# Softmax sums by f16 matmuls over each head's partitions, and four elementwise steps on GpSimd

## The chip, the cores and the metric

The kernel runs on one core of a Trainium2 chip. A core has a matrix engine (TensorE, PE in the profile), a vector engine (VectorE, DVE), an activation engine (ScalarE, ACT), GpSimd (POOL) and a queue that issues the DMAs (SyncE, SP). The metric is the device time of one execution in microseconds, less is better. The time before is the median of three runs, 1120.3 us.

## The reference

Eight sequences of 512 tokens, model width 512, 16 heads of 32, feed-forward width 2048. All inputs and outputs are float32. Cut to what matters:

```python
xn = layernorm(x)                       # over the last axis
q, k, v = heads(xn @ Wq.T), heads(xn @ Wk.T), heads(xn @ Wv.T)
q, k = rope(q), rope(k)
scores = einsum('bhqd,bhkd->bhqk', q, k) / sqrt(32), causal
attn = softmax(scores)                  # exp, divided by its sum over the keys
ctx = einsum('bhqk,bhkd->bhqd', attn, v)
s = ctx @ Wo.T
h = gelu(bitlinear(xn, w_fc))           # ternary weights
g = silu(bitlinear(h, w_proj))
out = x + s * g
```

The change is in the division by the softmax's sums.

## The kernel before

Work comes in units: 8 sequences x 4 groups of four heads make 32 units of attention (`attn(n)`), and 32 tiles of 128 tokens of the feed-forward part (`ffn`, then `out_tile`). The attention of unit n runs like this:

- `pqk`, 24 f16 matmuls (the inputs are split into an f16 hi and an f16 lo part, three products for each), then the rotation on VectorE into `r` (lines 842 to 847), its rounding `rh` on ScalarE and the rest `rl` on VectorE (851, 852). SP stores both through DRAM (`dq`, `dk`) and loads them back as stacked operands `qst` and `kst` (856 to 864).
- `pm`, 16 matmuls per unit for the row maxima. VectorE reduces them with a mask (line 886, `scr` in the profile), and the shifts go back into `qst`.
- `scores(kb)`, four blocks of 128 keys: `psc` matmuls, the exponential on ScalarE into the f32 tile `p{kb}` (four heads, only the queries from the block on), and the causal mask of its first 128 columns on GpSimd (`affine_select`, line 918). Keys are on the partitions, queries along the free axis.
- `weigh(kb)`: f32 matmuls of `v` (32 columns for each head) with `p{kb}` add up the context `cps` in a PSUM bank. The heads of a group lie at partitions 0, 32, 64 and 96 (`tile_position`).
- Gather (938 to 940): VectorE adds p1, p2 and p3 into p0, so that p0 holds, for every query, 128 partial sums. ScalarE copies `cps` to the SBUF tile `cu` (942).
- Sum (944 to 962): f32 matmuls of p0 with `sel`, 128 columns at a time, set the sums of the four query blocks into four rows of each head's 32 partitions, so that `sps` is 128 x 128. One reciprocal over 128 columns; its f16 hi and lo parts `rx`; eight f16 matmuls with `bsel` spread them over the head's partitions into `pbc` (128 x 512); VectorE multiplies `cu` by it.
- `chl` (964 to 967): the context's f16 hi part on ScalarE and lo part on VectorE, for the output matmuls `po` of `out_tile`.

The feed-forward part gives TensorE most of its work: `pf` (up), a gelu on ScalarE, `ghl` (hi and lo parts, ScalarE and VectorE), a transposing DMA `gT`, and `py` (down). `F` is the gate, `xr` the residual input and at last the output (line 1046, an addition on VectorE).

The order of the program isn't the order of the text. A planner (`Plan`) records every operation as a node with a cost (function `cost`) and a priority (`KEYS`, plus the unit's number), runs a list scheduling over the five engines, and emits the instructions in order of their planned starts. So every engine has a fixed order when it runs, and all instructions come from one line (439) in the profile; they are told apart by their tiles. `plan.join` makes one node of several matmuls. Its model of VectorE and GpSimd lengthens a GpSimd instruction that starts while VectorE runs one with two SBUF inputs (lines 380 to 384); a VectorE instruction isn't lengthened there by GpSimd.

Tiles come from pools with a fixed number of buffers: p0 to p3, `r`, `rh`, `rl`, `cu` and `rr` have one each, `cps` and `sps` one PSUM bank each, and six banks rotate for the other matmuls.

Of the kernel before, what the change touches and what calls it, by code (L numbers as in the profile page):

```python
# [21 lines left out]
P = 128  # L22
# [19 lines left out]
RBITS = 1597463007.0  # L42

KEYS = dict(
    e0=-0.253,
    e1=-2.644,
    e2=-1.78,
    e3=-0.65,
    e4=-0.087,
    e5=-0.039,  # L50
    lag=1.963,
    const0=-24.54,
    const1=-8.335,
    cst=-4.513,
    load=-2.111,
    stats=-22.226,
    norm=-1.897,
    factor=-4.454,
    wload=-1.833,
    wstep=1.494,  # L60
    weight=-19.388,
    balance=-4.407,
    wo=4.918,
    wfsum=-21.116,
    wf=-7.624,
    wp=-0.05,
    wpload=-1.337,
    wpsum=-14.152,
    tstep=0.06,
    proj=-0.686,  # L70
    rope=-24.912,
    hilo=-1.795,
    stack=-34.848,
    v=0.652,
    max=-0.869,
    shift=0.633,
    score=0.129,
    kstep=0.195,
    weigh=1.36,
    gather=1.125,  # L80
    sum=0.848,
    ctx=-41.941,
    up=-0.708,
    fstep=0.123,
    split=-0.465,
    root=0.15,
    down=0.339,
    gate=0.454,
    out=5.344,
    load0=-15.402,  # L90
    stats0=-12.949,
    norm0=-6.181,
    wload0=-7.484,
    weight0=-7.258,
    balance0=-15.07,
    wfload=-7.712,
)
TUNE = dict(table=5.421, margin=0, dma_margin=1734, reserve=0, window=2.34, wide=0.886, backlog=10530.0)

# [361 lines left out]
def cost(eng, op, out, ins, a, k):  # L461
    n, psum = out.n, any(x.store.where == "PSUM" for x in ins)
    if op == "dma_start":
        size = n * out.shape[0] * SIZE[out.dtype]
        t = 1310 if k.get("transpose") else 660 if size <= 16384 else 520
        return t, t, None
    if op == "matmul":
        m, n = ins[0], ins[1].n
        if SIZE[ins[1].dtype] == 4:
            t = n * 0.42 + 10 if m.n <= 32 else n * 4 / 2.4 + 20  # L470
        else:
            t = max(n / 2.4 + 2.5, 27.0)
        return t, t + 170, None
    if op == "transpose":
        return 110, 300, None
    if eng == "ACT":
        f = ins[0].n
        d = (160 if psum else 186) + 0.833 * f + 55 * (psum and f in (256, 384)) + 93 * sum(isinstance(k.get(q), View) for q in ("bias", "scale"))
        table = TABLE.get(a[2]) if op == "activation" else None
        if "accum_out" in k:  # L480
            return d + 100, d + 200, table
        return d - 95, d, table
    if eng == "POOL":
        full = sum(x.n == n for x in ins)
        if n <= 8:
            d = 110 if op == "memset" else 195 + 90 * (op == "tensor_scalar" and len(ins) > 1)
        elif op == "affine_select":
            d = 90 + 1.57 * n
        elif op == "memset":
            d = 100 + 0.84 * n  # L490
        else:
            d = 190 + 2.25 * n if full > 1 else 200 + 1.5 * n
        return d - 40, d, None
    if op == "tensor_tensor_reduce":
        d = 233 + 1.047 * n
    elif op == "reciprocal":
# [15 lines left out]
def block_kernel(  # L512
# [33 lines left out]
    def ps(shape, name, dt=F32):  # L546
        return pp(shape, dt, tag="ps", name=name)
# [18 lines left out]
    ones = cp([P, P], F32, name="ones")  # L566
    ident16 = cp([P, P], F16, name="ident16")
    mask = cp([P, S], BF16, name="mask")
    sel = cp([P, NT, DK], F32, name="sel")
    bsel = cp([P, NT, P], F16, name="bsel")  # L570
    kst = [cp([P, HG, S], F16, name=f"kst{i}") for i in range(2)]
    qst = [cp([P, HG, S], F16, name=f"qst{i}") for i in range(2)]
    rnd = cp([P, 2], F32, name="rnd")

    def constants():
        at("const0")
        ident = wk([P, P], F32, tag="rr", name="ident", bufs=1)
# [14 lines left out]
        for i in range(2):  # L592
            G.memset(kst[i][96:98].rearrange("p h s -> p (h s)").bitcast(F32), MSC2)
        G.memset(sel, 0.0)
        G.memset(sel[:, :, NT:], 1.0)
        for qb in range(NT):
            G.memset(sel[:, qb, qb : qb + 1], 1.0)
        G.memset(bsel, 1.0 / RSC)
        for qb in range(NT):
            v = bsel[:, qb, :].rearrange("p (j d) -> p j d", d=DK)  # L600
            G.affine_select(
                out=v, in_=v, pattern=[[-DK, HG], [0, DK]],
                compare_op=ALU.is_equal, fill=0.0, base=-qb, channel_multiplier=1,
            )
        at("cst")
        SP.dma_start(cst, cs.rearrange("t p s -> p t s"))

# [3 lines left out]
    def ln(b, ts):  # L611
# [25 lines left out]
        for i, t in enumerate(ts):  # L637
# [4 lines left out]
            tag, nb = ("hl", 3) if b else ("gT", 4)  # L642
            hl = wk([P, 2, D], F16, tag=tag, name=f"xhl{b}_{t}", bufs=nb)
            A.copy(hl[:, 0], xt)
            V.tensor_tensor(hl[:, 1], xt, hl[:, 0], ALU.subtract)
            flip(xT[b][:, :, :, t * P : (t + 1) * P], hl)
        at("factor", base)
        fs = wk([P, NT], F32, tag="fs", name=f"fs{b}_{ts[0]}", bufs=8)[:, 0:k]
# [45 lines left out]
    def out_weight():  # L694
# [21 lines left out]
        pb = pc([P, P], F32, tag="sps", name="pom2")[:, 0:2]  # L716
        T.matmul(pb, ones[0:1, :], r, start=True, stop=True)
        V.tensor_copy(cwo, pb)
        hi, lo = wo_s
# [12 lines left out]
    def tern_scale(which, acc, n):  # L732
        a1 = wk([P, 1], F32, tag="acc1", name=f"acc1{which}", bufs=2)
        V.tensor_reduce(a1, acc[:, 0:n], AX.X, ALU.add)
        pt = pc([P, P], F32, tag="sps", name=f"pacc{which}")[:, 0:1]
# [52 lines left out]
    def tern_down():  # L788
# [22 lines left out]
        ones16 = wk([P, P], F16, tag="rx", name="ones16", bufs=1)  # L811
        G.memset(ones16, 1.0)
        for i, w in enumerate(ws):
            at("wp", tstep=i)
# [9 lines left out]
    def attn(n):  # L824
# [24 lines left out]
        rh = wk([P, 2, S], F16, tag="rh", name=f"rh{n}", bufs=1)  # L849
        rl = wk([P, 2, S], F16, tag="rl", name=f"rl{n}", bufs=1)  # L850
        A.copy(rh, r)
        V.tensor_tensor(rl, r, rh, ALU.subtract)
        at("stack", n)
        q_, k_ = qst[n % 2], kst[n % 2]
        dqk = []
# [48 lines left out]
            )  # L904
        cps = pc([P, S], F32, tag="cps", name=f"cps{n}")
        isc = 1.0 / math.sqrt(DK)
        pts = {}

        def scores(kb):
            at("score", n, kstep=kb)  # L910
            w = S - kb * P
            pt = wk([P, HG, w], F32, tag=f"p{kb}", name=f"p{kb}_{n}", bufs=1)
            pts[kb] = pt
            for h in range(HG):
                p = ps([P, S], f"psc{n}_{kb}_{h}")
# [29 lines left out]
        for qb in range(NT):  # L945
# [12 lines left out]
        pb = ps([P, NT, P], f"pbc{n}")  # L958
        for qb in range(NT):
# [72 lines left out]
    def out_tile(b, t):  # L1032
# [71 lines left out]
```

## Time and profile before

| | |
|---|---|
| three runs | 1118.4, 1120.3, 1120.6 us |
| the profiled execution | 1119.6 us |
| its span, from the first to the last instruction | 1117.9 us |
| mean granted TensorE clock | 0.995 |

Where one unit's sums and division spend their time (mean of one instruction, from the groups by form):

| engine | instruction | in all | mean ns |
|---|---|---|---|
| PE | `sps`, f32 records, 32 x 128 columns | 1024 | 279 |
| PE | `pbc`, f16, 128 columns | 256 | 219 |
| PE | `cps`, f32 records, 512 / 384 / 256 / 128 columns | 1024 | 593 / 487 / 379 / 273 |
| VectorE | gather, 1536 / 1024 / 512 elements | 96 | 1778 / 1243 / 682 |
| VectorE | reciprocal, 128 x 128 | 32 | 955 |
| VectorE | `rx` hi / lo | 64 | 218 / 292 |
| VectorE | `cu` times `pbc` | 32 | 677 |
| VectorE | `rl` (1024) / `ch` (512) / `xhl` (512) / `xr` (512) | 128 | 1219 / 691 / 702 / 691 |
| ScalarE | copy of `cps` | 32 | 572 |
| GpSimd | causal mask of `p` | 512 | 422 |

How to read it: the profile lists, for each engine, how long its instructions ran. Matmuls overlap each other, so a record's own length (279 ns) is more than what it adds to the stream. An f32 matmul leaves two records, an f16 one a single record. Some matmul records can be missing.

### The profile page before, as it was taken

What the parts mean: (1) busy time and instruction counts of PE and PEld (TensorE: products, weight loads), DVE (VectorE), ACT (ScalarE), POOL (GpSimd) and SP (SyncE); (2) the same over time, 40 slices, a digit from 0 to 9 for tenths busy, and PEclk for the clock granted to TensorE, in tenths of its full rate; (3) what the DMA queues carried; (4) which work ended last, traced back from release to release, by engine and by line L of the source; (5) the groups of instructions that cost most, each with busy time, mean ns of one, the idle gap of its engine ahead of it and who ended that gap; (6) DMA issues with size and microseconds to landing.
All of it is one profiled execution on the core that took longest, in us unless ns stands there. A gap on an engine that the chain in (4) does not pass through costs nothing.

```text
span 1117.9 us, 23834 instructions
## 1 busy us (share of the span) xinstructions
PE 1077.2 (96%) x8118; PEld 559.3 (50%) x8118; DVE 881.3 (79%) x2187; ACT 698.9 (63%) x1519; POOL 533.6 (48%) x1661
## 2 busy tenths in 40 slices
PE   1899999999999999999999999999999999999998
PEld 0444554555455555455555455555455555545553
DVE  7999898987887777967787777886788777786754
ACT  6858865675566655567556557665557665555763
POOL 6487725542573336543363444643448333344452
PEclk9989999999999999999999999999999999999999
DMA  9875654553455434554545335452345543324423
GB/s 284 286 159 130 124 127 120 109 110 72 112 130 114 100 88 110 96 102 105 115 113 114 70 84 143 105 133 76 76 105 126 122 100 81 81 61 98 105 58 104
DMA packets 233178, 127.15 MB, mean 114 GB/s; under 512 B 191840, under 2 KB 208224, under 8 KB 233056
## 3 DMA queue, kind: packets, MB, share of 16 engines
q1 hardware_dynamic: 233056, 125.63, 48.2%
q8 instruction: 64, 1.05, 0.4%
q14 instruction: 58, 0.48, 0.1%
HBM read 55.05 MB, written 25.17 MB: 72 GB/s over the span
## 4 chain that ended last, share of the span: by engine, by line
PE 82%; DVE 8%; DMA 3%; POOL 3%; issue 2%; SPq 1%; ACT 1%; DVEq 0%
PE py L439 19%; PE pf L439 15%; PE pqk L439 13%; PE po L439 7%; PE pv L439 6%; PE psc L439 6%; PE pm L439 6%; PE cps L439 6%; PE sps L439 3%; POOL hu L439 2%; PE pbc L439 1%; POOL rs L439 1%; DMA wn<-in_wqk 1%; DVE p L439 1%; DVE r L439 1%
## 5 line engine op out<-in xcount | busy, mean ns | idle before, releaser
L439 PE MATMUL py<-wp,gT 128*128 128x512 f16 x1024 | 301.2, 379 | 0.0
L439 POOL TENSOR_SCALAR_AFFINE_SELECT p<-p 128x128 f32<-128x128 f32 x512 | 203.5, 422 | 115.4 <-ACT p L439 109.3
L439 ACT ACTIVATE p<-psc 128x256 f32<-128x256 f32 (+3 forms) x512 | 179.4, 450 | 118.8 <-PE psc L439 118.4
L439 PEld LDWEIGHTS <-xT 128*128 128x128 f16 x2560 | 186.4, 98 | 122.3 <-issue 11.1
L439 PE MATMUL pf<-wf,xT 128*128 128x512 f16 x1024 | 239.5, 380 | 1.3 <-ACT wf L439 1.3
L439 DVE CUSTOM_DVE_ANT_0 scr<-pm,mask 128x128 f16<-128x128 f32 (+3 forms) x512 | 221.3, 486 | 19.7 <-PE pm L439 18.4
L439 POOL TENSOR_TENSOR sq<-sq 128x1 f32<-128x1 f32 (+2 forms) x128 | 45.3, 354 | 346.8 <-ACT ghl L439 341.7
L439 PE MATMUL pqk<-xT,wqk 128*128 128x512 f16 x768 | 175.7, 382 | 0.0
L439 DVE TENSOR_TENSOR p<-p,p 128x1536 f32<-128x1536 f32 (+2 forms) x96 | 118.5, 1234 | 71.5 <-PE cps L439 61.1
L439 ACT CAST rh<-r 128x1024 f16<-128x1024 f32 x32 | 33.4, 1045 | 184.9 <-DVE r L439 179.6
L439 PEld LDWEIGHTS <-gT 128*128 128x128 f16 x1024 | 98.0, 97 | 94.8 <-issue 7.7
L439 DVE SCALAR_TENSOR_TENSOR ghl<-g,rng,ghl 128x512 f16<-128x512 f32 x128 | 95.5, 748 | 52.6 <-ACT ghl L439 50.9
L439 PE MATMUL pm<-kst,qst 96*128 96x128 f16 (+3 forms) x512 | 121.1, 303 | 2.7 <-DVE mm L439 0.9
L439 PE MATMUL psc<-qst,kst 98*128 98x256 f16 (+3 forms) x512 | 118.1, 299 | 0.4 <-DVE mm L439 0.2
L439 PEld LDWEIGHTS <-wqk 128*128 128x128 f16 x768 | 74.5, 99 | 86.7 <-issue 4.8
L439 ACT ACTIVATE g<-pf,fs 128x512 f32<-128x512 f32 x128 | 87.3, 683 | 36.7 <-PE pf L439 33.7
L439 PE MATMUL pv<-wv,xT 128*128 128x128 f16 x1536 | 95.3, 220 | 2.0 <-DMA wv<-whl 1.9
L439 ACT ACTIVATE ghl<-g,sq 128x512 f16<-128x512 f32 x128 | 91.6, 715 | 0.8 <-POOL sq L439 0.7
L439 ACT ACTIVATE ghl<-g,rng 128x512 f16<-128x512 f32 x128 | 91.5, 716 | 0.1
L439 PE MATMUL po<-wo,ch 128*128 128x512 f16 x384 | 88.3, 379 | 0.0
L439 ACT ACT_TABLE_LOAD x64 | 82.1, 1283 | 2.8 <-PE psc L439 1.0
L439 PE MATMUL cps<-p,v 128*32 128x512 f32 (+3 forms) x1024 | 83.3, 433 | 0.0
(141 smaller groups left out, 1343.7 us busy)
## 6 DMA issues: line engine op xcount, KB each, us to landing
qst<-dq SPq DMA_DIRECT2D x96, 128.0 KB, 3.0
kst<-dk SPq DMA_DIRECT2D x96, 128.0 KB, 3.1
xt<-in_x SPq DMA_DIRECT2D x32, 256.0 KB, 3.5
xr<-in_x SPq DMA_DIRECT2D x32, 256.0 KB, 3.0
out<-xr SPq DMA_DIRECT2D x32, 256.0 KB, 2.5
dq<-rh SPq DMA_DIRECT2D x32, 128.0 KB, 2.4
dk<-rh SPq DMA_DIRECT2D x32, 128.0 KB, 2.5
dq<-rl SPq DMA_DIRECT2D x32, 128.0 KB, 2.6
```

The costliest lines, as they stand in the source:

```text
L439: ins = getattr(self.real[nd.eng], op)(*[real(x) for x in a], **{q: real(x) for q, x in k.items()})
```

## The change

It does six things. (1) The sums are taken with a constant `tot` of 128 x 32, all 1/1024, over all 512 queries at once, so that each of a head's 32 partitions gets the same sum, divided by 1024 in the weight and multiplied by 1024 in the operand. For that the gathered p0 is split, in two halves of 256 queries, into an f16 hi part (ScalarE) and an f16 lo part (VectorE), which are put into the memory of p1 and p2; eight f16 matmuls add them up in `sps`, now 128 x 512. (2) The reciprocal runs over 512 columns and its result is what the context needs in each partition, so `rx`, `bsel` and `pbc` go. (3) The context is read from PSUM in the product, and the copy of `cps` goes. (4) Four steps go from VectorE to GpSimd: `rl`, the lo part of the context, the lo part `xhl` of the normalized input (for all sequences but the first), and the last addition into `xr`. (5) The planner's cost of an f16 matmul with 32 columns or fewer is a quarter of the former. (6) All priorities in `KEYS` and most values of `TUNE` are new, so that the order of the whole program is another. The constants `sel` and `bsel` are gone, and some small tiles lie under other tags.

```diff
-TUNE = dict(table=5.421, margin=0, dma_margin=1734, reserve=0, window=2.34, wide=0.886, backlog=10530.0)
+TUNE = dict(table=2.939, margin=1, dma_margin=1441, reserve=1, window=2.34, wide=0.883, backlog=15949.0)
...
-            t = max(n / 2.4 + 2.5, 27.0)
+            t = max(n / 2.4 + 2.5, 27.0) if m.n > 32 else max(n / 9.6 + 1.0, 27.0)
...
-    sel = cp([P, NT, DK], F32, name="sel")
-    bsel = cp([P, NT, P], F16, name="bsel")
+    tot = cp([P, DK], F16, name="tot")
...
+        G.memset(tot, 1.0 / RSC)
...
-            V.tensor_tensor(hl[:, 1], xt, hl[:, 0], ALU.subtract)
+            (G if b else V).tensor_tensor(hl[:, 1], xt, hl[:, 0], ALU.subtract)
...
-        V.tensor_tensor(rl, r, rh, ALU.subtract)
+        G.tensor_tensor(rl, r, rh, ALU.subtract)
...
-            pt = wk([P, HG, w], F32, tag=f"p{kb}", name=f"p{kb}_{n}", bufs=1)
+            raw[kb] = wk([P, 2 * HG * w], F16, tag=f"p{kb}", name=f"p{kb}_{n}", bufs=1)
+            pt = raw[kb].bitcast(F32).rearrange("p (h w) -> p h w", h=HG)
...
-        cu = wk([P, S], F32, tag="cu", name=f"cu{n}", bufs=1)
-        A.copy(cu, cps)
         at("sum", n)
-        sps = pc([P, P], F32, tag="sps", name=f"sps{n}")
-        for qb in range(NT):
-            plan.join = True
+        ahl = [raw[kb][:, 0 : HG * S].rearrange("p (h w) -> p h w", h=HG) for kb in (1, 2)]
+        for i in range(2):
+            hs = slice(i * S // 2, (i + 1) * S // 2)
+            A.activation(ahl[0][:, :, hs], pts[0][:, :, hs], AF.Copy, scale=RSC)
+            V.scalar_tensor_tensor(ahl[1][:, :, hs], pts[0][:, :, hs], RSC, ahl[0][:, :, hs], ALU.mult, ALU.subtract)
+        sps = pc([P, S], F32, tag="sps", name=f"sps{n}")
+        plan.join = True
+        for a in range(2):
             for h in range(HG):
                 T.matmul(
-                    sps[DK * h : DK * h + DK, :], sel[:, qb, :], pts[0][:, h, qb * P : (qb + 1) * P],
-                    start=(qb == 0), stop=(qb == NT - 1), tile_position=(0, DK * h),
+                    sps[DK * h : DK * h + DK, :], tot, ahl[a][:, h, :],
+                    start=(a == 0), stop=(a == 1), tile_position=(0, DK * h),
                 )
-            plan.join = None
-        rr = wk([P, P], F32, tag="rr", name=f"rr{n}", bufs=1)
+        plan.join = None
+        rr = wk([P, S], F32, tag="rr", name=f"rr{n}", bufs=1)
         V.reciprocal(rr, sps)
-        rx = wk([P, 2, P], F16, tag="rx", name=f"rx{n}", bufs=1)
-        V.tensor_scalar(rx[:, 0], rr, RSC, None, ALU.mult)
-        V.scalar_tensor_tensor(rx[:, 1], rr, RSC, rx[:, 0], ALU.mult, ALU.subtract)
-        pb = ps([P, NT, P], f"pbc{n}")
-        for qb in range(NT):
-            for a in range(2):
-                T.matmul(pb[:, qb, :], bsel[:, qb, :], rx[:, a], start=(a == 0), stop=(a == 1))
-        V.tensor_tensor(cu, cu, pb.rearrange("p a b -> p (a b)"), ALU.mult)
+        cu = wk([P, S], F32, tag="cu", name=f"cu{n}", bufs=1)
+        V.tensor_tensor(cu, cps, rr, ALU.mult)
...
-        V.tensor_tensor(chl[:, 1], cu, chl[:, 0], ALU.subtract)
+        G.tensor_tensor(chl[:, 1], cu, chl[:, 0], ALU.subtract)
...
-        V.tensor_tensor(xr, xr, F, ALU.add)
+        G.tensor_tensor(xr, xr, F, ALU.add)
```

More of the change, by code (lines that the diff above doesn't have):

```diff
@@ L44 @@
 KEYS = dict(
[L45 to L96, printed above, removed]
+    e0=-0.291,
+    e1=-2.232,
+    e2=-1.64,
+    e3=-0.189,
+    e4=-0.61,
+    e5=-0.034,
+    lag=2.012,
+    const0=-25.636,
+    const1=-9.365,
+    cst=-1.613,
+    load=-2.107,
+    stats=-18.101,
+    norm=-1.942,
+    factor=-0.587,
+    wload=-1.573,
+    wstep=1.536,
+    weight=-13.751,
+    balance=-3.455,
+    wo=4.776,
+    wfsum=-12.771,
+    wf=-6.783,
+    wp=-0.441,
+    wpload=-1.703,
+    wpsum=-3.384,
+    tstep=0.106,
+    proj=-0.618,
+    rope=-24.134,
+    hilo=-15.6,
+    stack=-28.295,
+    v=0.349,
+    max=-0.824,
+    shift=0.779,
+    score=0.142,
+    kstep=0.252,
+    weigh=0.16,
+    gather=0.681,
+    sum=1.245,
+    ctx=-37.701,
+    up=-0.632,
+    fstep=0.095,
+    split=-0.497,
+    root=0.632,
+    down=0.369,
+    gate=1.588,
+    out=5.026,
+    load0=-23.925,
+    stats0=-11.953,
+    norm0=-5.714,
+    wload0=-7.222,
+    weight0=-7.314,
+    balance0=-29.165,
+    wfload=-7.848,
 )
-TUNE = dict(table=5.421, margin=0, dma_margin=1734, reserve=0, window=2.34, wide=0.886, backlog=10530.0)
+TUNE = dict(table=2.939, margin=1, dma_margin=1441, reserve=1, window=2.34, wide=0.883, backlog=15949.0)
 SIZE = {F16: 2, BF16: 2, F32: 4, I32: 4}
@@ L576, in constants @@
         at("const0")
-        ident = wk([P, P], F32, tag="rr", name="ident", bufs=1)
+        ident = wk([P, S], F32, tag="cu", name="ident", bufs=1)[:, 0:P]
         G.memset(ident, 0.0)
@@ L593, in constants @@
             G.memset(kst[i][96:98].rearrange("p h s -> p (h s)").bitcast(F32), MSC2)
-        G.memset(sel, 0.0)
-        G.memset(sel[:, :, NT:], 1.0)
-        for qb in range(NT):
-            G.memset(sel[:, qb, qb : qb + 1], 1.0)
-        G.memset(bsel, 1.0 / RSC)
-        for qb in range(NT):
[L600 to L604, printed above, removed]
+        G.memset(tot, 1.0 / RSC)
         at("cst")
@@ L715, in out_weight @@
         V.reciprocal(r[:, 1:2], r[:, 0:1])
-        pb = pc([P, P], F32, tag="sps", name="pom2")[:, 0:2]
+        pb = pc([P, S], F32, tag="sps", name="pom2")[:, 0:2]
         T.matmul(pb, ones[0:1, :], r, start=True, stop=True)
@@ L734, in tern_scale @@
         V.tensor_reduce(a1, acc[:, 0:n], AX.X, ALU.add)
-        pt = pc([P, P], F32, tag="sps", name=f"pacc{which}")[:, 0:1]
+        pt = pc([P, S], F32, tag="sps", name=f"pacc{which}")[:, 0:1]
         T.matmul(pt, ones, a1, start=True, stop=True)
@@ L810, in tern_down @@
         tern_scale(1, acc, NW)
-        ones16 = wk([P, P], F16, tag="rx", name="ones16", bufs=1)
+        ones16 = wk([P, S], F16, tag="scr", name="ones16", bufs=2)[:, 0:P]
         G.memset(ones16, 1.0)
@@ L906, in attn @@
         isc = 1.0 / math.sqrt(DK)
-        pts = {}
+        pts, raw = {}, {}
         def scores(kb):
@@ L940, in attn @@
             V.tensor_tensor(acc, acc, pts[kb], ALU.add)
-        cu = wk([P, S], F32, tag="cu", name=f"cu{n}", bufs=1)
-        A.copy(cu, cps)
         at("sum", n)
-        sps = pc([P, P], F32, tag="sps", name=f"sps{n}")
-        for qb in range(NT):
-            plan.join = True
+        ahl = [raw[kb][:, 0 : HG * S].rearrange("p (h w) -> p h w", h=HG) for kb in (1, 2)]
[6 more added lines that the diff above has]
+        for a in range(2):
             for h in range(HG):
                 T.matmul(
-                    sps[DK * h : DK * h + DK, :], sel[:, qb, :], pts[0][:, h, qb * P : (qb + 1) * P],
-                    start=(qb == 0), stop=(qb == NT - 1), tile_position=(0, DK * h),
-                )
-            plan.join = None
-        rr = wk([P, P], F32, tag="rr", name=f"rr{n}", bufs=1)
+                    sps[DK * h : DK * h + DK, :], tot, ahl[a][:, h, :],
+                    start=(a == 0), stop=(a == 1), tile_position=(0, DK * h),
+                )
+        plan.join = None
+        rr = wk([P, S], F32, tag="rr", name=f"rr{n}", bufs=1)
         V.reciprocal(rr, sps)
-        rx = wk([P, 2, P], F16, tag="rx", name=f"rx{n}", bufs=1)
-        V.tensor_scalar(rx[:, 0], rr, RSC, None, ALU.mult)
-        V.scalar_tensor_tensor(rx[:, 1], rr, RSC, rx[:, 0], ALU.mult, ALU.subtract)
-        pb = ps([P, NT, P], f"pbc{n}")
-        for qb in range(NT):
-            for a in range(2):
-                T.matmul(pb[:, qb, :], bsel[:, qb, :], rx[:, a], start=(a == 0), stop=(a == 1))
-        V.tensor_tensor(cu, cu, pb.rearrange("p a b -> p (a b)"), ALU.mult)
+        cu = wk([P, S], F32, tag="cu", name=f"cu{n}", bufs=1)
+        V.tensor_tensor(cu, cps, rr, ALU.mult)
         at("ctx", n)
```

## The prediction

> **What bounds the kernel now.** I read the page first: busy shares, then the chain that ended last.
>
> ```profile
> PE 1077.2 (96%) x8118; PEld 559.3 (50%) x8118; DVE 881.3 (79%) x2187; ACT 698.9 (63%) x1519; POOL 533.6 (48%) x1661
> ...
> PE 82%; DVE 8%; DMA 3%; POOL 3%; issue 2%; SPq 1%; ACT 1%; DVEq 0%
> ```
>
> A busy TensorE need not be at its peak, so I asked for windows of 100 us (columns: window, length, then busy us of PE, PEld, DVE, ACT and POOL).
>
> ```profile
> 300.00:400.00 100.00, 99.26 (x758) 51.66 (x757) 78.99 (x196) 61.92 (x136) 48.61 (x155) 1.00 0.45 99
> 900.00:1000.00 100.00, 100.00 (x766) 52.67 (x765) 73.43 (x179) 59.58 (x132) 37.67 (x123) 1.00 0.37 88
> ```
>
> From 200 us to 1000 us PE loses at most 0.7 us in 100, and the granted clock is 1.00. TensorE's own stream is the bound: an instruction less on PE shortens the run, and a wait of PE lengthens it. Next, the PE timeline of one unit (start, length of a group of alike instructions; the next group's start tells what it occupied).
>
> ```profile
> 613.03 0.86 PE L439 MATMUL sps<-p,sel 128*32 128x128 f32 x24
> 613.71 0.83 PE L439 MATMUL cps<-p,v 128*32 128x256 f32 x16
> 614.48 1.47 PE L439 MATMUL pf<-wf,xT 128*128 128x512 f16 x6
> ...
> 627.91 0.43 PE L439 MATMUL sps<-p,sel 128*32 128x128 f32 x8
> 628.15 1.69 PE L439 MATMUL cps<-p,v 128*32 128x512 f32 x16
> 629.77 0.34 PE L439 MATMUL psc<-qst,kst 98*128 98x128 f16 x3
> ```
>
> The f32 work lies in two batches: 1.45 us for 384 sps and 384 cps columns (each of four heads), 1.86 us for 128 and 896. The difference gives 0.41/256 = 1.60 ns a column, and 0.22 us is left over per batch, which I take as the price of entering and leaving it. Last, what a long GpSimd instruction does to VectorE; before the change the only such ones in the attention part are the weights' lo parts, whl.
>
> ```profile
> 101.37 1.42 POOL L439 TENSOR_TENSOR whl<-wn,whl 128x512 f16<-128x512 f32 x1 [1.58 <-ACT wn L439]
> 101.76 1.57 DVE L439 SCALAR_TENSOR_TENSOR ghl<-g,rng,ghl 128x512 f16<-128x512 f32 x1
> ...
> 103.26 0.68 DVE L439 TENSOR_TENSOR p<-p,p 128x512 f32<-128x512 f32 x1
> ...
> 103.99 0.30 PE L439 MATMUL sps<-p,sel 128*32 128x128 f32 x2 [0.77 <-DVE p L439]
> ```
>
> That ghl has a mean of 748 ns; here it took 1.57 us and ended 0.5 us after whl. The gather behind it on VectorE came late, and PE stood 0.77 us at sps. At 111.99 a second ghl lasted 1.40 us behind a whl, while mask reductions, which read PSUM, ran beside another whl at 0.55 and 0.69 us. So what waits is VectorE's work with two SBUF inputs.
>
> **The change, part by part** (32 units of batch and head group).
>
> PE removes. The sums: 512 columns x 1.60 = 0.82 us. The broadcast pbc: 0.06 + 0.39 us in the timeline, 0.45. Together 1.27 us a unit, 40.7 us.
>
> PE adds eight f16 matmuls of 512 columns, 32 wide. No row has this form. Far bound above: one after another as the wide ones (12 in 2.59 us, so 0.216 each), 1.73 us. Nearer: the f32 records of cps, eight to four heads, follow each other every 0.10 us though one of 512 columns lasts 593 ns, so the column groups run side by side; f16 needs one record where f32 has two, which bounds a group of four at 0.41 us. Below, one wide matmul, 0.216. I take 0.22, two groups, 0.44 us a unit, 14.1 us (to 55). Batches: in the order of the built kernels, runs of f32 matmuls rise from 75 to 97, since cps now comes in three pieces, and 32 runs of f16 sums join them: 54 x 0.22 = 11.9 us (from 0). PE's sum: -40.7 + 14.1 + 11.9 = -15 us, between -27 and +27.
>
> VectorE loses, by mean rows: rl 1.22, xhl 0.70 (28 tiles), ch 0.69, xr 0.69, the 128-wide reciprocal 0.96, both rx 0.51, the cu product 0.68: 5.4 us. It gains two hi/lo subtractions of 1024 elements (row rl, 1.22 each), the product from PSUM (0.68), and a reciprocal of 512. Its bounds: 0.96 (no growth) and 3.8 (four times the row); the rows of 1 element (152 ns) and of 128 (955) give 6.3 ns an element, 3.4 us, which I take. Net +1.1 us, so about 36 us more on 881: some 81% of the span, no bound by itself. ScalarE loses the cu copy (0.57) and gains two copies of 1024 (rh's row, 1.05): +49 us, 66%, hidden by its idle time (it waits 180 us for r); without that cover, 1.5 us a unit.
>
> GpSimd gains rl, ch, xhl and xr, 124 instructions. From whl (median 1157 ns at 512) and z (220 ns at one element): 1.16 us each, rl 2.1 us; +173 us, 63% of the span. Behind rl on its queue stand the sq and z steps, which the gate needs much later. SP's loads of qst and kst stand behind the dq and dk stores of rl, which land perhaps 1 to 2 us later; pm follows r by 12 us today and is what would be late. The output's DMA follows xr by 0.5 us; th waits for its buffer (3.3 us in all today).
> The sel and bsel constants leave GpSimd's start, where it waits 6.5 us for wn anyway: nothing.
>
> What GpSimd's long instructions cost VectorE is the unknown. In the built order, two of four units run: last gather, first subtraction, second subtraction, reciprocal, with ScalarE doing rh ahead of the second half's copy. Counting from the end of r: gather to 0.6, subtraction to 1.75; rh to 1.05, copy to 2.1. rl wants to start at 1.1, gets in at about 1.7 and runs to 3.8. The second subtraction, ready at 2.1, starts at 3.7: 1.6 us late. Then sps is late, on which PE stands, and reciprocal, ghl and the masks are queued behind it on VectorE. The reciprocal is ordered ahead of a ghl that is ready some 2.4 us after that copy (ScalarE's g, 0.68 + 0.19, its Square, 0.72 + 0.19, its copy, 0.72, one running into the next), so the plan has at most 0.5 us of room at sps: 1.1 us a unit, 16 units, 18 us. In the other two, rl falls under the reciprocal or under the statistics of the next batch, which have one input: 0. The last xhl of a batch comes behind the last masks, where the gathers are: 0.9 us in 8 units, 7 us. ch and xr fall under masks: 0. Bounds: 0 if all is covered; by the whl rows (1.3 us of PE waits for p, from three such instructions after 100 us), 0.43 us x 156 lengths of 512 = 68 us. I take 25, nearer to the lower end, because the order shows where they fall; 1150 in the range stands for 45.
>
> The Trainium skill, "SBUF — State Buffer", section "SBUF: two separate sides", calls the port pair of VectorE and GpSimd an exclusive lock: whichever starts first holds it for its whole instruction. The rows above show the wait, but ghl came through at 0.82 and 0.65 us extra, parts of a whl. By the rule taken at its worst, every one of the 156 lengths would cost its full 1.16 us of VectorE, 181 us, and the run would pass 1280; by the rows it is the 25 above.
>
> Sum: the profiled execution took 1119.6 us (span 1117.9), 0.7 under the median. 1117.9 - 15 + 25 = 1128 us of span, 1130 as a median.
>
> **The rivals.**
> 1. Faster: the waits are covered and only PE's saving counts. For it: DVE idles 20 us in 100, and PE chooses among plenty of matmuls of the feed-forward part. Against: the order is fixed when built, and it already puts sps where its input comes. 1120.3 - 15 = 1105; with 5 us of waits or the batches at nothing, 1094 to 1110. It decides where PE loses under 0.47 us a unit (15/32).
> 2. Even: waits near 15 us, 1118 to 1122.5.
> 3. The f16 column groups don't run side by side: PE +27 us, 1147, and more with waits. The overlapping f32 records speak against it.
> 4. The long reciprocal: sps to cu grows by 2.4 us and the single cps bank is held until then. By the built order the next cps starts about 10 us of PE work after sps, against some 5.5 us of reciprocal, ghl and product; 1 us a unit beyond that gives 1105 + 32 = 1137.
>
> **How the numbers follow.** Forecast (waits over 17 us, up to 45: 1122.5 to 1150) 0.45; rival 1, 0.38; rival 2, 0.07; rivals 3 and 4, 0.05 each. What a measurement can tell from no change is about 0.2%, 2.2 us. Slower 0.45 + 0.05 + 0.05 = 0.55, same 0.07, faster 0.38. The range must reach into rival 1: 1095 to 1150, leaving out about 0.2; the forecast's own range is 1122.5 to 1150.
>
> **What would show it.** Right: pbc gone and eight sps records a unit in about 0.5 us; PE waiting at sps for p (some 1 us, in half of the units), with a subtraction of 2.5 us or more beside rl; PE idle of 2 to 3 us in 100. Wrong: PE as dense as before and a batch's period, now 133.0 us (pqk at 464.22 and 597.20), shorter by 1.8 us; or sps taking 1.7 us; or VectorE's two-input instructions at their old durations beside rl, which would take the whole price away.

## The result and the profile after

| | before | after |
|---|---|---|
| median of four runs each | 1119.35 us | 1135.3 us |
| lowest to highest | 1118.07 to 1120.6 | 1134.91 to 1136.52 |
| span of the profiled execution | 1117.9 us | 1133.2 us |
| mean granted TensorE clock | 0.995 | 0.993 |

The ratio is 1.0144, with a 95% interval of 1.0127 to 1.0162: slower by 1.4%. The page of the profile after, in the two lines shown of before (busy time by engine, then the chain that ended last by engine):

```profile
PE 1068.3 (94%) x7094; PEld 516.6 (46%) x7094; DVE 967.7 (85%) x2063; ACT 753.6 (67%) x1553; POOL 734.5 (65%) x1775
...
PE 66%; DVE 15%; POOL 7%; ACT 4%; DMA 4%; issue 3%; SPq 1%; POOLq 0%; DVEq 0%; ACTq 0%
```

TensorE works 8.9 us less, as meant, and the run is 15.3 us longer. VectorE, with 15% of the chain instead of 8%, and GpSimd, with 7% instead of 3%, now end more of the waits. The two windows of 100 us that were shown of before (window, length, busy PE, PEld, DVE, ACT, POOL, clock):

```profile
300.00:400.00 100.00, 98.09 (x664) 47.94 (x663) 87.20 (x183) 67.00 (x143) 70.27 (x169) 1.00 0.49 112
900.00:1000.00 100.00, 100.00 (x710) 50.15 (x708) 84.43 (x171) 64.97 (x137) 55.17 (x136) 1.00 0.40 95
```

The late window is as dense as before; the early one lost 1.2 us more. The groups by form show what the new instructions cost (form, count, then total us and mean ns, then idle time of the engine ahead of them):

```profile
L439 DVE RECIPROCAL rr<-sps 128x512 f32<-128x512 f32 x32 | 107.3, 3353 | 8.7 <-PE sps L439 8.5
L439 PE MATMUL sps<-p,tot 128*32 128x512 f16 x256 | 21.8, 389 | 5.2 <-DVE p L439 3.2 <-ACT p L439 2.0
L439 DVE SCALAR_TENSOR_TENSOR p<-p,p 128x1024 f16<-128x1024 f32 x64 | 99.5, 1565 | 5.6 <-ACT p L439 5.2 <-PE cps L439 0.2
L439 POOL TENSOR_TENSOR rl<-r,rh 128x1024 f16<-128x1024 f32 x32 | 81.3, 2542 | 103.7 <-ACT rh L439 103.7
L439 POOL TENSOR_TENSOR ch<-cu,ch 128x512 f16<-128x512 f32 x32 | 43.9, 1372 | 46.1 <-ACT ch L439 46.1
```

The wide reciprocal is 3.35 us, the eight f16 matmuls overlap (256 of them are 21.8 us busy), and the subtraction of 1024 elements is longer in the mean than the 1.22 us that the same size took before: some of these instructions were held up. PE's timeline of a unit (start, length) has the pattern that was forecast, with a wait for p in the middle of the sums, but a short one:

```profile
633.40 0.40 PE L439 MATMUL sps<-p,tot 128*32 128x512 f16 x4
634.01 0.40 PE L439 MATMUL sps<-p,tot 128*32 128x512 f16 x4 [0.21 <-DVE p L439]
634.35 1.47 PE L439 MATMUL po<-wo,ch 128*128 128x512 f16 x6
```

Where was the time lost? The starts of the reciprocals serve as marks, one for each unit of attention:

| stretch, between the reciprocals' starts (units counted from 0) | before | after | difference |
|---|---|---|---|
| start to unit 0 | 104.5 us | 122.4 us | +17.9 |
| unit 0 to unit 8 | 242.9 | 248.1 | +5.1 |
| unit 8 to unit 24, four batches | 532.5 (133.1 a batch) | 528.0 (132.0 a batch) | -4.5 |
| unit 24 to unit 31 | 214.9 | 212.2 | -2.7 |
| unit 31 to the end | 23.1 | 22.5 | -0.6 |

All of the loss, 23.0 us, lies ahead of unit 8, in the first two of the eight batches. The steady batches, for which the prediction's sum was made, became shorter by 1.1 us. PE's longest waits of the whole run (us in all, times, longest):

```profile
PE pacc L439 <- DVE acc L439: 22.0, 1, 22.0
PE po L439 <- POOL ch L439: 7.1, 5, 1.7
PE pf L439 <- ACT wf L439: 4.9, 1, 4.9
PE sps L439 <- DVE p L439: 3.2, 7, 1.1
```

The first, at the very start, was there before (21.6 us). The wait of the output matmuls for GpSimd's `ch`, which the prediction put at nothing, is over twice PE's wait at sps for VectorE's p, which it put at 18 us (3.2 us; another 2.0 us at sps were for ScalarE's hi part).

### The profile page after: what moved, and what is told of

Same layout as the page of the kernel before. It is cut to its first block, busy times and chain, and to the rows that moved or that the text cites. A ratio compares the mean times of both kernels' runs of the same rounds, so it can differ in the third digit from the quotient of the medians.

```text
span 1133.2 us, 21760 instructions
## 1 busy us (share of the span) xinstructions
PE 1068.3 (94%) x7094; PEld 516.6 (46%) x7094; DVE 967.7 (85%) x2063; ACT 753.6 (67%) x1553; POOL 734.5 (65%) x1775
## 4 chain that ended last, share of the span: by engine, by line
PE 66%; DVE 15%; POOL 7%; ACT 4%; DMA 4%; issue 3%; SPq 1%; POOLq 0%; DVEq 0%; ACTq 0%
PE py L439 16%; PE pqk L439 11%; PE pf L439 11%; PE pm L439 6%; PE po L439 6%; PE cps L439 5%; PE psc L439 5%; PE pv L439 5%; DVE p L439 5%; POOL hu L439 3%; DVE r L439 2%; DVE t L439 2%; ACT p L439 2%; POOL rs L439 2%; DMA wn<-in_wqk 1%
## 5 line engine op out<-in xcount | busy, mean ns | idle before, releaser
L439 PE MATMUL py<-wp,gT 128*128 128x512 f16 x1024 | 288.3, 379 | 0.0
L439 POOL TENSOR_SCALAR_AFFINE_SELECT p<-p 128x128 f32<-128x128 f32 x512 | 228.0, 473 | 85.0 <-ACT p L439 81.3
L439 ACT ACTIVATE p<-psc 128x256 f32<-128x256 f32 (+3 forms) x512 | 181.4, 455 | 111.8 <-PE psc L439 104.5
L439 PE MATMUL pqk<-xT,wqk 128*128 128x512 f16 x768 | 193.8, 382 | 0.1
L439 DVE TENSOR_TENSOR p<-p,p 128x1536 f32<-128x1536 f32 (+2 forms) x96 | 126.8, 1321 | 32.3 <-POOL p L439 26.9
L439 POOL TENSOR_TENSOR rl<-r,rh 128x1024 f16<-128x1024 f32 x32 | 81.3, 2542 | 103.7 <-ACT rh L439 103.7
L439 PE MATMUL psc<-qst,kst 98*128 98x256 f16 (+3 forms) x512 | 130.8, 302 | 3.8 <-ACT g L439 1.6
L439 DVE RECIPROCAL rr<-sps 128x512 f32<-128x512 f32 x32 | 107.3, 3353 | 8.7 <-PE sps L439 8.5
L439 ACT ACTIVATE ghl<-g,sq 128x512 f16<-128x512 f32 x128 | 91.6, 716 | 27.3 <-POOL sq L439 21.8
L439 DVE SCALAR_TENSOR_TENSOR p<-p,p 128x1024 f16<-128x1024 f32 x64 | 99.5, 1565 | 5.6 <-ACT p L439 5.2
L439 PE MATMUL cps<-p,v 128*32 128x512 f32 (+3 forms) x1024 | 94.0, 442 | 0.6 <-POOL p L439 0.6
L439 ACT ACTIVATE p<-p 128x1024 f16<-128x1024 f32 x64 | 67.5, 1055 | 37.6 <-DVE p L439 37.4
```

The source lines that it names most:

```text
L439: ins = getattr(self.real[nd.eng], op)(*[real(x) for x in a], **{q: real(x) for q, x in k.items()})
```

## The experiments

Three questions were open: what the sums alone are worth, what GpSimd's four steps cost and through what, and why the start lost so much. "Before" is always the median in the same job, 1120 to 1122 us.

### Parts of the change, planned anew

The first six kernels change one part of the source and let the planner make a new order from it. Two of them divide the change in two. `e3_sums_only` has the new sums, with the four steps on VectorE and the old priorities:

```diff
-            (G if b else V).tensor_tensor(hl[:, 1], xt, hl[:, 0], ALU.subtract)
+            V.tensor_tensor(hl[:, 1], xt, hl[:, 0], ALU.subtract)
...
-        G.tensor_tensor(rl, r, rh, ALU.subtract)
+        V.tensor_tensor(rl, r, rh, ALU.subtract)
```

and the same for `ch` and `xr`, with KEYS and TUNE of before.

> The changed kernel's sums (f16 hi and lo, 512-wide reciprocal, product from PSUM) with the four steps on VectorE and the priorities of the kernel before. Port theory: TensorE's saving without GpSimd's holding, 1104 to 1116. Load theory: VectorE has 33 us a unit to do in under 33, so 1140 or more. Order theory: 1105 to 1115.

Measured: 1382.0 us, ratio 1.2323 (1.2296 to 1.2351).

`e2_lo_on_gpsimd_only` is the kernel before with the four steps on GpSimd (the same four lines the other way round) and its own priorities.

> The kernel before with only the four steps moved to GpSimd, its own priorities. VectorE gets 3.2 us a unit less to do. Port theory: slower than before, 1125 to 1145, with PE waits for p, rl or ch. Load theory: the same as before or faster, 1112 to 1120. Order theory: near before, 1115 to 1125.

Measured: 1164.9 us, 1.0394 (1.0378 to 1.041).

`e5_new_priorities_only` is the kernel before with nothing but the changed kernel's KEYS and TUNE.

> The kernel before with nothing changed but the priorities and planner settings of the changed kernel. Order theory: the first reciprocal comes 10 us or more later than the 104.5 us of before, and the run takes 1130 or more. Port and load theories: within 6 us of before, 1114 to 1126.

Measured: 1265.3 us, 1.1284 (1.1264 to 1.1303).

`e1_lo_on_vector` is the changed kernel with the four steps on VectorE, as in the diff above, and its own priorities.

> The changed kernel with all four steps back on VectorE, its own priorities, planned anew. Port theory: 1115 to 1130. Load theory: 1140 to 1180, VectorE over 90% busy. Order theory: 1130 to 1145.

Measured: 1215.3 us, 1.0847 (1.0828 to 1.0865).

`e8_first_on_vector` puts the steps on VectorE for the first two batches alone:

```diff
-        G.tensor_tensor(rl, r, rh, ALU.subtract)
+        (G if n >= 8 else V).tensor_tensor(rl, r, rh, ALU.subtract)
```

(`ch` likewise; `xhl` from the third batch on and `xr` from the second on GpSimd).

> The changed kernel with the four steps on VectorE for the first two sequences and on GpSimd from the third on. Port theory, with the loss in the first 250 us: the start gets 10 us or more back, 1116 to 1126. Load theory: the start gets worse, 1138 to 1150. Order theory: 1130 to 1140.

Measured: 1289.4 us, 1.1501 (1.1475 to 1.1526).

`e9_planner_lock` changes only the planner's model: it learns that a long GpSimd instruction holds VectorE's two-input ones.

```diff
             if e == "DVE" and nd.lock:
+                st = max(st, pheld - 138)
                 held = st + nd.dur
...
+            elif e == "POOL" and nd.wide_pool:
+                pheld = st + occ
```

> The changed kernel, its planner told that a VectorE instruction with two SBUF inputs can't start before a long GpSimd one is done. The work is the same, the order is planned around the waits. Port theory: part of the waits is avoided, 1118 to 1130. Load theory: 1130 to 1140, since the work of each engine is the same. Order theory: anything from 1115 to 1150, since the order is another.

Measured: 1238.2 us, 1.1047 (1.1028 to 1.1067).

What follows: none of these six measures what it was made for. `e5_new_priorities_only` computes exactly what the kernel before computes, on the same engines, and loses 13%; its steady part shows what a poor order looks like (400 us; PE idle 18 us of them, and a granted clock of 0.92 in place of 1.00):

```profile
600.00:1000.00 400.00, 381.86 (x2549) 181.19 (x2551) 272.95 (x681) 215.02 (x458) 159.48 (x521) 0.92 0.40 90
```

An edit of this program comes with a new order. `e5_new_priorities_only` (13% against before) and `e9_planner_lock` (9% against the changed kernel) do the same work as the kernels they are compared with, so there the order alone cost up to ten times what was to be measured; in the other four, which lost 4 to 23% against before, order and edit can't be told apart. That the better model of the lock lost 9% is a miss of the theory behind it, that the planner only lacked the knowledge. The rest of the study starts from the changed kernel's order, instruction by instruction; all but the last run keep it and change only how single steps are issued.

### The same order, four steps on VectorE or as zeros

The planner plans the changed kernel as it is; only when the instructions are written out, marked steps go to VectorE at their places or become one GpSimd memset, which writes zeros (so the three lo parts and the last addition are left out):

```diff
-                ins = getattr(self.real[nd.eng], op)(
+                eng = self.real[nd.eng]
+                if nd.emit_as == "DVE":
+                    eng = self.real["DVE"]
+                elif nd.emit_as == "ZERO":
+                    op, a, k = "memset", (a[0], 0.0), {}
+                ins = getattr(eng, op)(
```

> The changed kernel with its instruction order kept as it is; the four steps on GpSimd (rl, ch lo, xhl lo, xr) are replaced by writing zeros there, which reads no SBUF and takes about half as long. The lo parts and the output are zero, so that part of the work is left out. Port theory (GpSimd's two-input instructions hold up VectorE's two-input ones): the second subtraction and the gathers go back to 1.22 and 1.78 us and the run falls to 1105 to 1118. Load theory (the start is bound by VectorE's and ScalarE's own extra work): 1128 or more. Order theory (the new priorities make a bad start): 1128 to 1136.

Measured (`e7_zero_same_order`): 1110.3 us, 0.9901 (0.9886 to 0.9917); span 1108.6, a batch 129.8 us, the reciprocal of unit 8 at 355.48 us (347.43 before, 370.46 after).

> The changed kernel with its planned order kept, but the four steps issued by VectorE at their places in that order. VectorE gets some 3.2 us a unit more, GpSimd's long instructions are gone. Port theory: the gain from the freed port is larger than the added work only where VectorE has room, so 1120 to 1135. Load theory: slower than 1135, 1140 to 1180, with VectorE over 90% busy. Order theory: about 1135 to 1145.

Measured (`e6_vector_same_order`): 1132.5 us, 1.0093 (1.0074 to 1.0113); a batch 132.4 us, unit 8 at 368.57 us. VectorE is busy 89% of the span.

What follows: the four steps on GpSimd cost 25.0 us against zeros (1135.3 - 1110.3), 15.0 of it ahead of unit 8 and 8.7 in the four steady batches. On VectorE, at the same places, they cost 22.2. Putting them on GpSimd thus gained nothing in this order: the ratios to before, 1.0144 and 1.0093, have intervals that don't meet. With the four steps left out the program is 1% faster than before. That is no price of the new sums alone: the kernel before does these four steps on VectorE, and its order is another.

### Time on GpSimd, or what it reads

`e10_two_memsets` keeps GpSimd about as long busy with each step as the real one, but reads nothing:

```diff
+                elif nd.emit_as == "TWO":
+                    op, a, k = "memset", (a[0], 0.0), {}
+                    ins = eng.memset(real(a[0]), 0.0)
+                    self.tc.keep_in_program_order(ins)
```

> The changed kernel in its own order; each of GpSimd's four new steps (rl, xhl after the first batch, ch, xr) is issued as two memsets of the same tile, which leaves the lo parts and the output's addition out. One memset of rl took 0.95 us and one of the others 0.52, so a pair takes about 1.9 and 1.05 us, near the 2.5 and 1.2 to 1.4 us of the real steps, but reads nothing in SBUF; it also doesn't wait for its inputs. Theory A (the 24.6 us between the changed kernel and the one with single memsets are VectorE's, held up while GpSimd reads two operands): the subtraction 1024 stays at 1.23 us, and the time is 1109 to 1116 us. Theory B (they are GpSimd's own: its queue is longer, and ch and xhl come late from it whatever VectorE does): 1122 to 1133 us, with PE still waiting more than 1 us for ch.

Measured: 1112.8 us, 0.9919 (0.9895 to 0.9943). The groups by form of this run:

```profile
L448 DVE SCALAR_TENSOR_TENSOR p<-p,p 128x1024 f16<-128x1024 f32 x64 | 77.7, 1224 | 5.1 <-ACT p L448 4.6 <-PE cps L448 0.2
...
L448 POOL MEMSET rl<- 128x1024 f16 x32 | 30.4, 951 | 1.8
L446 POOL MEMSET rl<- 128x1024 f16 x32 | 30.3, 947 | 0.0
```

VectorE's subtraction is back at 1.22 us although GpSimd is at work for 1.9 us in place of rl. The time is 2.5 us above that with single memsets, within the spread of its own runs (1108.3 to 1113.4), and 22.5 below the changed kernel: as theory A forecast. One thing this run doesn't separate: a memset waits for no input, while in the changed kernel rl stands 103.7 us in all at the head of GpSimd's queue, waiting for rh (the group above). So a part of the 22.5 us can still be GpSimd's queue, and not what VectorE waits for.

### One step at a time

`e11_rl_zero` and `e12_ch_zero` use the "ZERO" form for rl alone and for ch alone.

> The changed kernel in its own order with rl alone replaced by one memset (its lo part is left out); xhl, ch and xr stay as they are. By the prediction's split (18 of 25 us from rl beside the second subtraction) the run takes 1135 - 18 = about 1117 us. By the trace of the steady state, where the late subtraction cost only about 0.4 us at sps because sps had some 2 us of room, rl is worth 0.4 us in half of the units there and some part of the 15 us before the ninth unit: 1125 to 1133 us.

Measured: 1121.8 us, 1.0006 (0.9994 to 1.0018). rl is worth 13.5 us by the medians and 11.5 by the spans of the profiled executions (1133.2 and 1121.7). The medians are from two jobs, whose medians of before differ by 1.3 us, so such differences are good to a microsecond or two.

> The changed kernel in its own order with the lo part of ch alone replaced by one memset (left out); rl, xhl and xr stay. The prediction put ch at 0: 1134 to 1136 us. By the trace, PE waited 7.1 us for ch in five units, 1.3 us of it in the first unit of each steady batch (GpSimd has its gate steps ahead of ch and takes 1.15 us for it): 1125 to 1130 us, and the steady batches 1.3 us shorter (132.0 to 130.7 us).

Measured: 1129.2 us, 1.0075 (1.006 to 1.0091). ch is worth 6.1 us (5.8 by the spans). What is left of the 25.0, 5.4, goes to xhl and xr, if the parts add up; these two weren't run alone.

The reciprocals' distances within a steady batch tell where (units 11 to 15, us):

| | 11 to 12 | 12 to 13 | 13 to 14 | 14 to 15 | batch |
|---|---|---|---|---|---|
| after | 33.01 | 31.04 | 30.88 | 37.08 | 132.01 |
| rl as zeros | 32.07 | 31.04 | 30.88 | 36.77 | 130.76 |
| ch as zeros | 32.35 | 31.05 | 30.88 | 37.08 | 131.36 |
| all four as zeros | 31.15 | 31.04 | 30.88 | 36.77 | 129.84 |

The prediction's place is easily found in the timeline of unit 12, after:

```profile
498.75 2.12 POOL L439 TENSOR_TENSOR rl<-r,rh 128x1024 f16<-128x1024 f32 x1
498.78 3.18 DVE L439 SCALAR_TENSOR_TENSOR p<-p,p 128x1024 f16<-128x1024 f32 x1 [0.21 <-ACT p L439]
...
501.40 0.40 PE L439 MATMUL sps<-p,tot 128*32 128x512 f16 x4
...
502.01 0.40 PE L439 MATMUL sps<-p,tot 128*32 128x512 f16 x4 [0.21 <-DVE p L439]
...
502.34 1.47 PE L439 MATMUL po<-wo,ch 128*128 128x512 f16 x6
502.46 3.36 DVE L439 RECIPROCAL rr<-sps 128x512 f32<-128x512 f32 x1 [0.50 <-PE sps L439]
```

The second subtraction started 0.03 us behind rl and took 3.18 us, in the place that was forecast. With rl as zeros, in the same unit:

```profile
491.77 1.23 DVE L444 SCALAR_TENSOR_TENSOR p<-p,p 128x1024 f16<-128x1024 f32 x1 [0.21 <-ACT p L444]
...
494.40 0.61 PE L444 MATMUL sps<-p,tot 128*32 128x512 f16 x8
494.95 1.25 PE L444 MATMUL po<-wo,ch 128*128 128x512 f16 x5
495.07 3.36 DVE L444 RECIPROCAL rr<-sps 128x512 f32<-128x512 f32 x1 [2.07 <-PE sps L444]
```

The reciprocal waits 2.07 us for PE, which comes to sps only 1.4 us after the subtraction has ended, and to the four matmuls that need its result some 0.3 us later. So of 1.95 us of lateness only a part reached PE: from the first sps to the matmul behind the sums it took 0.94 us (501.40 to 502.34) in place of 0.55 (494.40 to 494.95), 0.39 us, of which the profile shows 0.21 as a wait. The other late subtraction of the batch (530.15, 2.74 us, unit 13) reached PE with nothing, and the distances 12 to 13 and 13 to 14 are the same in all four rows to 0.01 us. What rl costs a steady batch (1.25 us) is in the first and the last column. The last one begins with the statistics of the next batch (timeline after, then with rl as zeros):

```profile
594.66 2.13 POOL L439 TENSOR_TENSOR rl<-r,rh 128x1024 f16<-128x1024 f32 x1 [3.51 <-ACT rh L439]
594.69 0.66 DVE L439 BATCH_NORM_STATS2 st<-xt 128x6 f32<-128x512 f32 x1
...
595.93 0.89 DVE L439 TENSOR_SCALAR ab<-mv 128x2 f32<-128x2 f32 x1
...
597.10 0.75 POOL L439 TENSOR_SCALAR hu<-ab 128x4 f32<-128x4 f32 x1 [0.31 <-DVE ab L439]
```

```profile
588.53 0.15 DVE L444 TENSOR_SCALAR ab<-mv 128x2 f32<-128x2 f32 x1
...
588.97 0.76 POOL L444 TENSOR_SCALAR hu<-ab 128x4 f32<-128x4 f32 x1 [4.34 <-DVE ab L444]
```

The statistics themselves run beside rl at their old 0.66 us, but a step over two elements, with one input from SBUF, took 0.89 us in place of 0.15: it ended at 596.82, just after rl (596.79). The chain of small GpSimd steps (`hu`, then `sq` and `z` for the gate) hangs on it, and ch stands behind that chain. But `hu` stands in GpSimd's queue behind rl too, which ended at 596.79. Against PE's stream, which ran 7.4 us apart in the two runs there, `hu` came 0.7 us later than with zeros (597.10 and 588.97); it waited only the last 0.31 us for ab. Either alone would have made it late, rl's place in the queue until 596.79 and ab until 597.10, and no run separates the two. The chain then ran almost without a gap up to ch. After, and with rl as zeros:

```profile
606.02 0.62 ACT L439 CAST ch<-cu 128x512 f16<-128x512 f32 x1 [0.26 <-DVE cu L439]
...
607.13 0.97 POOL L439 TENSOR_SCALAR z<-sq,rng 128x1 f32<-128x1 f32 x1
...
608.65 1.15 POOL L439 TENSOR_TENSOR ch<-cu,ch 128x512 f16<-128x512 f32 x1
...
609.85 0.60 PE L439 MATMUL po<-wo,ch 128*128 128x512 f16 x2 [1.34 <-POOL ch L439]
```

```profile
599.87 1.46 POOL L444 TENSOR_TENSOR ch<-cu,ch 128x512 f16<-128x512 f32 x1
...
601.39 0.61 PE L444 MATMUL po<-wo,ch 128*128 128x512 f16 x2 [0.38 <-POOL ch L444]
```

The cast of ch ended at 606.64, but GpSimd, with the gate's steps first, took ch up at 608.65 and PE stood 1.34 us. With rl as zeros ch starts 6.1 us behind the reciprocal instead of 7.2, and PE waits 0.38, 0.96 less. Matching PE's matmuls of the two runs one by one from 469 to 603 us gives nearly the whole account of the 1.25 us: 0.96 at this step's po (477.85 in that batch), of which 0.2 is made up by the next cps, 0.37 at the sums of unit 12, and 0.11 at the sums of unit 15.

### All the work, placed by hand

The last kernel leaves nothing out. Behind the planner's order, it moves rl, where a second subtraction follows within 3.5 us, to VectorE behind that subtraction, and ch ahead of the gate's steps:

```diff
+        for nd in [x for x in order if x.role == "rl"]:
+            i = order.index(nd)
+            j = next((j for j in range(i, len(order)) if order[j].role == "sub1"), None)
+            if j is not None and order[j].start - nd.start < 3500:
+                nd.eng = "DVE"
+                defer(i, j)
```

> All work of the changed kernel, TensorE's, ScalarE's and SyncE's order kept. In the 22 units where a hi/lo subtraction of the sums stands within 3.5 us behind rl, rl goes to VectorE, behind the second subtraction, where VectorE waits for sps (2.2 us at the reciprocal at 615.16 us of the run with zeros); the other ten stay on GpSimd. On GpSimd ch goes ahead of the gate's steps that stood up to 1 us before its cast. Theory (the price is where the two-operand steps fall, not that they are there): rl's 13.6 us come back nearly whole, and of ch's 6.1 us the 1.3 us a batch that PE waited: 1113 to 1121 us, a batch 130.0 to 130.8 us instead of 132.0, no subtraction over 1.3 us in the steady part. Rival (VectorE's load decides: all four steps on VectorE in the same order took 1132.5 us): the 27 us more on VectorE and the later rl put the reciprocal and pm later, 1126 to 1134 us.

Measured: 1140.4 us, 1.0178 (1.0163 to 1.0192). A miss for the theory, and the worst of the same-order runs; the rival's range ended at 1134 and missed it too. The waits that were aimed at are gone but for one: the subtraction is 1.25 us in the mean (one of 3.15 us is left, beside an rl that stayed on GpSimd), and PE no longer waits for GpSimd's ch between 400 and 1000 us. Others took their place. PE's waits of that stretch, and the timeline of unit 15:

```profile
PE pm L460 <- DMA kst<-dk: 5.6, 4, 1.6
PE sps L460 <- DVE p L460: 1.7, 1, 1.7
```

```profile
602.54 0.60 SPq L460 DMA_DIRECT2D dk<-rl  x1
605.03 0.81 SPq L460 DMA_DIRECT2D kst<-dk  x2
...
608.37 0.39 SPq L460 DMA_DIRECT2D kst<-dk  x1
...
610.88 0.33 PE L460 MATMUL pm<-kst,qst 96*128 96x128 f16 x2 [1.59 <-DMA kst<-dk]
```

dk's store of rl was issued 0.06 us ahead of the reciprocal's start (602.60), where the changed kernel has it 4.0 us ahead (597.44 and 601.46). The loads behind it came late in turn, and pm, which had waited for nothing there, stood 1.59 us. At unit 12 ch ahead of the gate held GpSimd idle for 3.48 us until the cast, and the gate's sq came 5.0 us later than in the changed kernel (509.21 and 504.21). A batch takes 133.4 us, 1.4 more than after. No version ran here that does all the work and beats the kernel before.

### The start

The table of stretches says that 23 us were lost ahead of unit 8. With all four steps as zeros 8.1 of them remain; the other 15.0 go with the four steps (6.2 of it rl and 3.0 ch, by unit 8's reciprocal in the runs with one step as zeros). On VectorE, in the same order, they cost nearly as much there, 13.1 us (368.57 against 355.48). Behind the 15.0 stand PE's waits and a lower clock. Windows from unit 0's reciprocal to 170 us, after, then with zeros:

```profile
122.40:170.00 47.60, 44.04 (x319) 21.75 (x317) 45.12 (x70) 24.73 (x54) 29.13 (x71) 0.93 0.44 99
121.86:170.00 48.14, 47.88 (x355) 23.94 (x353) 45.67 (x80) 32.53 (x70) 21.75 (x72) 1.00 0.47 114
```

Up to unit 8's reciprocal PE was idle for 16.2 us after and 7.4 with zeros, which is 8.8 of the 15.0. The granted clock was 0.93 here and 0.97 from 220 to 270 us after, and 0.97 from 170 to 220 us with zeros; an estimate from these shares gives 4.8 us lost by the clock after and 1.5 with zeros, 3.3 more of the 15.0. Of the 8.1, one wait is visible: PE at the first pf for ScalarE's wf, 1.3 us before, 4.9 after, 8.7 with zeros. The new order puts the weights' preparation and the first reciprocal (104.5 us before; 122.4 after, 121.9 with zeros) elsewhere; that the 8.1 us are the order's is likely, but no run separates it from the new sums. Whether a different order of the start would keep the gain of the steady part wasn't tried; the six replanned kernels show how little a guess at priorities is worth.

## Why the prediction was right or wrong, point by point

The time (1130 forecast, 1135.3 measured) and the sign were right. By the spans of the profiled executions, the change without the four steps is worth -9.3 us (1117.9 to 1108.6; forecast -15) and the four steps cost 24.6 (1108.6 to 1133.2; forecast 25). The terms of the sum came out as follows.

- TensorE's saving, forecast at -15 us: mechanism right, size too small. With PE never waiting (400.00 us busy of 400 with zeros), a batch is 129.84 us, against 133.12 before with some 0.47 of idle (398.58 us busy of 400): 0.70 us a unit, not 0.46. sps takes 0.54 us in the stream (501.43 to 501.97 in the last run), near the 0.44 assumed. The term that was mis-sized is the 0.22 us for entering and leaving a batch of f32 matmuls, 11.9 us: 1.27 - 0.54 is 0.73, so the measured 0.70 leaves 0.03 x 32, about 1 us, for it. From start to start of PE's matmuls in the steady batches, cps did take 0.19 us a unit more than before, but the other matmuls took 0.16 less. A remainder of two equations had been taken for a price.
- "The f16 column groups run side by side": right, and rival 3 is out. The reciprocal at 3.35 us (3.4 forecast): right; no wait for the cps bank is among PE's waits, so rival 4 is out as well.
- VectorE's load, forecast at 881 + 36 = 917 us: 926.8 with zeros, where the four steps don't hold it, and 967.7 after; the 41 us between are instructions made longer and not work.
- GpSimd's price, forecast at 25 us: measured 25.0. rl is 13.5 (forecast 18), ch 6.1 (0), xhl and xr 5.4 (7 and 0). The total is right partly by luck, since the working behind it failed in two places.
- "The plan has at most 0.5 us of room at sps: 1.1 us a unit": failed. The subtractions late by 1.5 to 2 us appear where they were forecast, in two of the four units of a steady batch, 13 in the run; but some 1.6 us of room was there in the order that ran (1.95 late, 0.39 at PE), since PE had other matmuls ahead of sps, and the second late subtraction of a batch cost nothing. So the sums lost about 0.4 us in one unit of four, 0.1 a unit, not 1.1 in every second. In 400 to 1000 us all waits of PE for p are 0.9 us, where the step has some 10.
- "In the other two, rl falls ... under the statistics of the next batch, which have one input: 0": failed, and this is where most of rl's steady price is, some 0.75 of 1.25 us a batch (the rest is at the sums). The statistics weren't held, but the small step ab behind them was, 0.74 us, and hu, which needs ab, stood behind rl on GpSimd as well; either was enough to make the chain late that ends in ch. The rule drawn from whl ("VectorE's work with two SBUF inputs") was too narrow.
- "ch and xr fall under masks: 0": failed for ch. The price isn't VectorE's: PE waits for ch itself, which stands last in GpSimd's queue, behind the gate's steps, and takes 1.15 us for 0.69. The prediction asked what is queued behind rl (and put it at nothing), and not what ch is queued behind.
- The sum was made for steady batches alone. The start wasn't in it, and there the change lost 15.0 us by GpSimd's steps and 8.1 by what is left without them, most likely its order; per unit the steps cost 1.9 us ahead of unit 8 and 0.54 in the steady part. What hid the working's errors is that a steady gain of 1.1 us a batch stood against a start that lost 23.
- Rival 1 (1105, waits covered) describes the run with zeros (1110) well: the saving on TensorE is real, in the steady batches at least, where PE never waits. It decides at 0.47 us of loss a unit by the prediction; with 25 us, or 0.78 a unit, and the start, it fell.

The Trainium skill's page "SBUF — State Buffer", section "SBUF: two separate sides", names two kinds of VectorE work that the lock excludes: those with two SBUF inputs against a GpSimd instruction that reads, and those in a two-port mode of its own. The prediction read only the first kind. That ab was held agrees with the second, and no run here shows in which mode ab ran. The 181 us that the rule gave at its worst are far off: VectorE's instructions became 41 us longer in all, and the run 25.0.

## What to carry to other kernels

Work moved to an engine with idle time costs three things that its busy share doesn't show: what it holds up elsewhere while it runs, what stands behind it in its queue, and what it stands behind; here the second was put at nothing and the third overlooked. Follow each moved result to its consumer, and read the room there from what the consumer's engine has to do ahead of it in the order that will run. Where a program's order is computed, test a part by changing the issue of single steps within a fixed order; a fresh order can cost ten times the effect.

## What the runs showed of the hardware

- A VectorE instruction over two elements (ab, 128x2 f32, one input) took 0.89 us beside a GpSimd subtraction and 0.15 us with rl as zeros. Statistics of 512 elements (674 and 676 ns in the mean) and mask reductions from PSUM (686 and 686 ns at 512) kept their times in these two runs.
- Two GpSimd memsets of rl, which read nothing, ran from 477.71 to 479.67 us in `e10_two_memsets` and left the VectorE subtraction of two SBUF inputs beside them (477.76) at 1.22 us; after, a GpSimd subtraction of 1024 elements that started 0.03 us ahead of it made it 3.18 us.
- The same work in a poorer order was granted a lower clock: 0.92 over 400 us with PE 95% busy, where the kernel before had 1.00 at 99.6% busy. Why, no run here tells.
